# Scanning the last turn of a batch in two halves of positions, in a hybrid of selective scan, attention and experts

## The chip, the cores and the metric

The kernel runs on one core of one Trainium2 chip. The metric is the device time of one execution in microseconds (us). Beside it a profile is taken: one execution recorded by the hardware profiler, from which all the views below are answered. The engines are PE (TensorE: matmuls, and PEld for its weight loads), DVE (VectorE), ACT (ScalarE), POOL (GpSimd) and SP (SyncE, which here issues nearly all DMAs).

## The reference

The input x is 4 x 384 x 32 x 32 (batch, channels, height, width). Layer 0 is a selective scan in four directions over the 1024 positions; layer 1 is windowed causal attention and a mixture of four experts, of which each token takes two.

```
xs = _cross_scan(gn(x))          # 4 directions: rows, columns, and both reversed
h  = h * exp(dt * A) + (dt * u) * B_t     # per channel, 16 states, over 1024 positions
y  = sum over states of h * C_t
x  = x + gelu(layernorm(y0 + y2 reversed + (y1 + y3 reversed) transposed))
t  = tokens of x                 # 4 x 1024 tokens of 384
t  = t + attention(ln(t))        # 6 heads, causal, the last 64 positions
t  = t + experts(ln(t))          # softmax gate, top 2 of 4, 384 -> 1536 -> 384
```

A token needs y at its position from all four directions of its batch. It does not need y at later positions.

## The kernel before, in words

**Order of instructions.** Nothing is ordered by hand. Every stage is a Python generator that yields either a condition or an instruction (lines 137 to 204). `Machine` (218 to 382) runs all of them in a modelled time, with a cost for each instruction, and emits the instructions of each engine in the order in which its model would start them; `bias` makes a stage early (-6 us) or late (+6 us). On the chip each engine then runs its own list in that order and waits for semaphores.

**The scan.** One (batch, direction) is a *turn*, `turns` at 562: 16 turns, four per batch, in the order of directions 1, 3, 0, 2 (`ORDER`, 560; odd ones go by columns, 2 and 3 are reversed). The 384 channels are three tiles t of 128, each four groups j of 32; 32 channels x 4 states fill the 128 partitions. A *block* is (turn, t, j), 12 per turn, and a block has four groups g of states. So there are 48 *slots* per turn and 768 in all, taken by pairs of blocks (`place_of`, 574). A slot is

- `times_b` (814): POOL multiplies dt*u (tile dtus) by B (tile bcs) into z, 128x1024;
- `decay` (830): ACT makes dA = exp(a * dt), in PSUM, two buffers;
- `scan` (856): DVE runs `tensor_tensor_scan` along the 1024 positions, into z or into dA;
- `times_c` (843): POOL or DVE, whichever the model has freer, multiplies by C into z;
- `fold_y` (890), once per two blocks: PE sums the states with a matrix of ones (`fold`) into a PSUM bank, and the 128x512 result is added to what lies in DRAM (`ydr`, laid out as tile t, group j, 64 rows of half and channel, 512 positions).

`spread` (804) loads dt and dt*u from DRAM (`dtr`, four buffers) with each row repeated for four states; `time_steps` (764) makes them on PE, ACT and DVE some 40 slots ahead; `state_rows` (752) loads B and C.

**The tokens.** `tokens(b)` (967) handles eight tiles of 128 tokens, three at a time, with four weight buffers of 576 KB (of the eight that the experts also use) and row buffers out of ten. It starts when `layer1` (1516) sees ("scan", b), which `fold_y` sets after the batch's last fold (927). A tile loads its rows of y (991) and x, and goes through two normalizations, q/k/v, attention, projection, a third normalization, and the gate's logits.

**The experts.** `routes` (1521) sorts each half batch (four token tiles) to experts: `route` (1212) scatters rows by indirect DMA; a half batch becomes 5 or 14 tiles of 128 rows (`SIZES`, 43), 19 a batch. `loads`, `hidden`, `gelus` and `output` (1371 to 1451) run these tiles in order: weights in 576 KB pieces, `ps_hid` and `y_ff` matmuls. `combine` (1464) gathers and adds. All of it is spawned late.

So scans of batch b+1 run beside tokens and experts of batch b, on the same in-order engines; after the last scan only the tokens and experts of batch 3 and what is left of batch 2's experts remain.

Of the kernel before, what the change touches and what calls it, by code (L numbers as in the profile page):

```python
# [11 lines left out]
F32 = mybir.dt.float32  # L12
AF = mybir.ActivationFunctionType
ALU = mybir.AluOpType
# [3 lines left out]
P = 128  # L18
B, D, HH, WW = 4, 384, 32, 32
L = HH * WW  # L20
T = D // P
HB = 512
NH = L // HB
KG, NS, R = 4, 16, 12
# [4 lines left out]
JB = P // 32  # L29
NB = T * JB  # L30
SG = 4
NG = NS // SG
# [7 lines left out]
PT = NT // 2  # L40
# [18 lines left out]
def bcast(ap, n):  # L59

    return ap.unsqueeze(1).to_broadcast([ap.shape[0], n, ap.shape[1]])
# [331 lines left out]
def conv_attn_hybrid(  # L393
# [8 lines left out]
    const = ctx.enter_context(tc.tile_pool(name="const", bufs=1))  # L402
# [77 lines left out]
    count_p = const.tile([P, SEG], F32, name="count_p")  # L480
    base_e = const.tile([P, NE], F32, name="base_e")
    a4 = const.tile([P, KG, T, JB, NG], F32, name="a4")

    m = Machine(nc)
    ps_a = ctx.enter_context(tc.tile_pool(name="ps_a", bufs=1, space=PSUM))
# [65 lines left out]
    ydr = [dram.tile([T, JB, P // 2, LH], F32, tag="ydr", name="ydr") for _ in range(B)]  # L551
# [5 lines left out]
    wl2 = dram.tile([NE, NCH, P, HT * D], F32, name="wl2", bufs=1)  # L557
    pwl = dram.tile([P, T * D], F32, name="pwl", bufs=1)

    ORDER = (1, 3, 0, 2)  # L560
    LAST_BY_COLUMNS = 3
    turns = [(b, ORDER[ki]) for b in range(B) for ki in range(KG)]
    blocks = [(i, t, j) for i in range(len(turns)) for t in range(T) for j in range(JB)]
    NSLOT = len(blocks) * NG
    SP = 2 * NG
    TS, IS = JB * NG, NB * NG
    AHEAD = 3
    xds, dtws, bcs, dtrs, spreads = {}, {}, {}, {}, {}
    zs, das, ready = {}, {}, set()
    have = set()  # L570
    count_of = dict(scan=0, times=0)
    pe, act, dve, pool, sp = m.pe, m.act, m.dve, m.pool, m.sp

    def place_of(s):

        return s // SP * 2 + s % 2, s % SP // 2

    def scans(n):
        return lambda: count_of["scan"] >= n
# [184 lines left out]
    def time_steps():  # L764

        for i, (b, k) in enumerate(turns):
            for t in range(T):
                yield lambda: i in xds and ("u", b) in have and count_of["scan"] >= (i * T + t) * TS - 40
                u = yield from us_all.take("ub")
                yield from sp.dma_start(u, udr[b][t])  # L770


                dtr = dram.tile([2, P, L], F32, tag="dtr", name="dtr", bufs=4)
                bias = dtb_sb[:, k, t : t + 1]
                for h in range(NH):
                    c, r = ts(h, HB), slice(32 * h, 32 * h + R)
                    e, dt = yield from eds.take("ed", n=2)
                    w = yield from banks.take("ps_dt", 0)
                    yield from pe.matmul(w, dtws[i][r, ts(t, P)], xds[i][r], start=True, stop=True)
                    yield from act.activation(e, w, AF.Abs, bias=bias)  # L780
                    yield from act.activation(dt, w, AF.Relu, bias=bias)
                    yield from act.activation(e, e, AF.Exp, scale=-1.0)
                    yield from act.activation(w, e, AF.Identity, bias=1.0)
                    yield from dve.scalar_tensor_tensor(e, w, -1.0, e, ALU.add, ALU.subtract)
                    yield from act.activation(w, w, AF.Ln)
                    yield from dve.tensor_tensor(w, w, e, ALU.subtract)
                    yield from dve.tensor_tensor(w, w, dt, ALU.add)
                    if k % 2:
                        v = slice(h * (WW // NH), (h + 1) * (WW // NH))
                        yield from dve.tensor_tensor(  # L790
                            e.rearrange("p (w h) -> p w h", h=HH),
                            w.rearrange("p (w h) -> p w h", h=HH), colmajor(u)[:, v, :], ALU.mult,
                        )
                    else:
                        yield from dve.tensor_tensor(e, w, u[:, c], ALU.mult)
                    yield from act.copy(dt, w)
                    banks.give(w)
                    yield from sp.dma_start(dtr[1][:, c], e)
                    yield from sp.dma_start(dtr[0][:, c], dt)
                    eds.give(e, dt)  # L800
                us_all.give(u)
                dtrs[i, t] = dtr

    def spread(c):

        for n, (i, t, j) in enumerate(blocks):
            yield lambda: (i, t) in dtrs
            dst = yield from (dtus if c else dts).take("dts")
            yield from sp.dma_start(
                dst, dtrs[i, t][c, 32 * j : 32 * j + 32, :].unsqueeze(1).to_broadcast([32, SG, L])  # L810
            )
            spreads[n, c] = dst

    def times_b():
        for s in range(NSLOT):
            n, g = place_of(s)
            i = blocks[n][0]
            yield lambda: (
                (n, 1) in spreads and (i, g, 0) in bcs and s <= count_of["scan"] + AHEAD
            )  # L820
            z = yield from zs_.take("z", 0)
            yield from pool.tensor_tensor(z, spreads[n, 1], bcs[i, g, 0], ALU.mult)
            zs[s] = z
            count_of["times"] += 1
            if g == NG - 1:
                dtus.give(spreads.pop((n, 1)))
            if n % NB == NB - 1:
                bs_.give(bcs.pop((i, g, 0)))

    def decay():  # L830
        for s in range(NSLOT):
            n, g = place_of(s)
            i, t, j = blocks[n]
            yield lambda: (n, 0) in spreads
            da = yield from das_.take("dA")
            yield from act.activation(
                da, spreads[n, 0], AF.Exp, scale=a4[:, turns[i][1], t, j, g : g + 1]
            )
            das[s] = da
            if g == NG - 1:  # L840
                dts.give(spreads.pop((n, 0)))

    def times_c(s, h, on_pool):
        n, g = place_of(s)
        i = blocks[n][0]
        yield lambda: (i, g, 1) in bcs
        if on_pool:
            yield from pool.tensor_tensor(zs[s], zs[s], bcs[i, g, 1], ALU.mult)
        else:
            yield from dve.tensor_tensor(zs[s], h, bcs[i, g, 1], ALU.mult)  # L850
            das_.give(h)
        if n % NB == NB - 1:
            cs_.give(bcs.pop((i, g, 1)))
        ready.add(s)

    def scan():

        for s in range(NSLOT):
            n, g = place_of(s)
            i = blocks[n][0]  # L860
            yield lambda: s in zs and s in das
            z, da = zs[s], das.pop(s)
            on_pool = count_of["times"] >= min(s + AHEAD, NSLOT) and m.clock["pool"] < m.clock["dve"] + LEAD
            h = z if on_pool else da
            if turns[i][1] >= 2:
                yield from dve.tensor_tensor_scan(
                    h[:, ::-1], da[:, ::-1], z[:, ::-1], 0.0, ALU.mult, ALU.add
                )
            else:
                yield from dve.tensor_tensor_scan(h, da, z, 0.0, ALU.mult, ALU.add)  # L870
            count_of["scan"] = s + 1
            if s % SP == 0:
                m.spawn(fold_y(n), EARLY)
            if on_pool:
                das_.give(da)
                m.spawn(times_c(s, h, True))
            else:
                yield from times_c(s, h, False)
        ended.append(True)
        yield lambda: len(das_.free) == 2  # L880
        for n in range(2):
            banks.free.append(das_.free.pop(0))
        for stock, n in ((zs_, NZ), (dts, 4), (dtus, 4)):
            yield lambda: len(stock.free) == n
            rows.free += stock.free
            stock.free = []
# [3 lines left out]
    def fold_y(n):  # L890


        i, t, j = blocks[n]
        b, k = turns[i]
        rows_y = ydr[b][t, j : j + 2].rearrange("j r l -> (j r) l")
        prev = yield from yps.take("yp")
        yield from sp.dma_start(prev, rows_y)
        ps = None
        for g in range(NG):
            s = n // 2 * SP + 2 * g  # L900
# [22 lines left out]
        banks.give(ps)  # L923
        yield from sp.dma_start(rows_y, prev)
        yps.give(prev)
        folded[b] = folded.get(b, 0) + 2
        if folded[b] == KG * NB:
            have.add(("scan", b))

    folded = {}  # L930

# [35 lines left out]
    def tokens(b):  # L967
# [3 lines left out]
        scale = 1.0 / float(np.sqrt(HD))  # L971
        p = rp.tile([P, NT, NE], F32, tag="p", name="p", bufs=B)
# [11 lines left out]
        wp = yield from weights("wp", pwl.rearrange("p (t o) -> p t o", t=T))  # L984

        def tile(a):
            w = yield from rows.take("yl")
            tt = yield from rows.take("tt")
            hf, r = divmod(a, NT // 2)
# [525 lines left out]

    def layer1():
        for b in range(B):
            yield lambda: ("scan", b) in have
            yield from tokens(b)

    def routes():
# [76 lines left out]
```

## Time and profile before

| what | us |
|---|---|
| median of 3 runs | 3890.63 (3870.85 to 3907.89) |
| the profiled execution | 3882.5, span 3880.8 |
| PE busy | 3033.4 (78%) |
| DVE busy | 2940.7 (76%) |
| POOL busy | 2824.4 (73%) |
| ACT busy | 2226.8 (57%) |
| start of the last scan | 3201.87 |
| mean granted TensorE clock | 0.822 |

Busy shares are means over stages that differ; a share of 78% says little by itself. The page cuts the span into 40 slices of 97 us, and the windows view gives each engine's busy time in any stretch, also for one tile's instructions alone. A group's line gives its busy time, the mean duration of one in ns, and the idle time of its engine just before it with what ended that.

Two numbers of batch 1 (batches are counted from 0 here) help to follow the text. In the timeline its token tiles' first loads (yl) are issued at 1597 us and its fourth token tile's logits stand at 1938.10.

### The profile page before, as it was taken

What the parts mean: (1) busy time and instruction counts of PE and PEld (TensorE: products, weight loads), DVE (VectorE), ACT (ScalarE), POOL (GpSimd) and SP (SyncE); (2) the same over time, 40 slices, a digit from 0 to 9 for tenths busy, and PEclk for the clock granted to TensorE, in tenths of its full rate; (3) what the DMA queues carried; (4) which work ended last, traced back from release to release, by engine and by line L of the source; (5) the groups of instructions that cost most, each with busy time, mean ns of one, the idle gap of its engine ahead of it and who ended that gap; (6) DMA issues with size and microseconds to landing.
All of it is one profiled execution on the core that took longest, in us unless ns stands there. A gap on an engine that the chain in (4) does not pass through costs nothing. (4 is left out here: it accounts for less than half of the span.)

```text
span 3880.8 us, 50273 instructions
## 1 busy us (share of the span) xinstructions
PE 3033.4 (78%) x15868; PEld 1841.7 (47%) x15868; DVE 2940.7 (76%) x3358; ACT 2226.8 (57%) x4017; POOL 2824.4 (73%) x1474
## 2 busy tenths in 40 slices
PE   2555555577697988777768889899787899998997
PEld 1100010045464555344345545566555557876886
DVE  2999999998888998888888899988788992332001
ACT  2545454467586777755557767778675763432221
POOL 1999989988898877888888699889787981012001
PEclk6555556678798999876678989899898999998997
DMA  5775775544478998734357989776568975459995
GB/s 202 266 273 204 270 268 203 174 143 149 171 253 333 341 374 324 285 127 164 112 208 254 329 301 347 270 254 213 203 228 295 388 272 184 136 167 327 318 318 182
DMA packets 394145, 953.65 MB, mean 246 GB/s; under 512 B 49620, under 2 KB 173400, under 8 KB 393880
## 3 DMA queue, kind: packets, MB, share of 16 engines
q1 hardware_dynamic: 385688, 925.27, 68.1%
q0 software_dynamic: 8192, 25.17, 1.9%
q8 instruction: 126, 2.06, 0.2%
q14 instruction: 139, 1.14, 0.1%
HBM read 786.39 MB, written 182.78 MB: 250 GB/s over the span
## 5 line engine op out<-in xcount | busy, mean ns | idle before, releaser
L148 POOL TENSOR_TENSOR z<-dts,bc 128x1024 f32<-128x1024 f32 x768 | 1792.9, 2359 | 186.7 <-PE ps_y L159 105.8
L148 ACT ACTIVATE dA<-dts,a 128x1024 f32<-128x1024 f32 x768 | 854.6, 1118 | 536.8 <-DVE z L148 512.1
L159 PE MATMUL ps_y<-z,fold 128*32 128x512 f32 x3072 | 725.8, 765 | 436.2 <-POOL z L148 237.2
L148 DVE TENSOR_TENSOR_SCAN dA<-dA,z 128x1024 f32<-128x1024 f32 x409 | 935.6, 2288 | 93.2 <-ACT dA L148 77.7
L148 POOL TENSOR_TENSOR z<-z,bc 128x1024 f32<-128x1024 f32 x359 | 841.7, 2355 | 110.8 <-DVE z L148 96.2
L148 DVE TENSOR_TENSOR_SCAN z<-dA,z 128x1024 f32<-128x1024 f32 x359 | 807.8, 2276 | 31.6 <-ACT dA L148 28.6
L159 PEld LDWEIGHTS ps_hid<-xbt,w_sb 128*128 128x128 f32 x5472 | 667.0, 198 | 137.2 <-issue 38.3
L159 PE MATMUL y_ff<-w_sb,hs 128*128 128x384 f32 x1824 | 680.8, 515 | 58.5 <-ACT hs L159 46.4
L159 PE MATMUL ps_hid<-xbt,w_sb 128*128 128x128 f32 x5472 | 692.0, 284 | 33.1 <-ACT hs L148 8.2
L148 DVE TENSOR_TENSOR z<-dA,bc 128x1024 f32<-128x1024 f32 x409 | 499.1, 1220 | 13.8 <-DVE dA L148 0.5
L159 PEld LDWEIGHTS ps_y<-z,fold 128*32 128x32 f32 x3072 | 93.1, 120 | 872.8 <-POOL z L148 412.8
L148 ACT ACTIVATE hs<-ps_hid,bb 128x128 f32<-128x128 f32 x912 | 274.1, 365 | 391.8 <-PE ps_hid L159 320.2
L159 PEld LDWEIGHTS y_ff<-w_sb,hs 128*128 128x128 f32 x1824 | 341.3, 199 | 314.9 <-issue 65.9
L148 POOL DMA_INDIRECT cb<-ysdr,idx x64 | 62.6, 979 | 293.7 <-DMA ysdr<-yb 269.8
L159 POOL TENSOR_TENSOR rn<-rn,half 128x1 f32<-128x1 f32 x96 | 52.7, 549 | 266.7 <-DVE rn L159 209.0
L148 DVE COPY yb<-y_ff 128x384 f32<-128x384 f32 x22 | 12.2, 556 | 251.5 <-PE y_ff L159 204.9
L148 POOL DMA_INDIRECT xsdr<-tks,idx x64 | 65.2, 1018 | 146.5 <-DVE idx L159 58.4
L148 ACT ACTIVATE ed<-ps_dt,dtb_sb 128x512 f32<-128x512 f32 x192 | 125.8, 681 | 67.6 <-PE ps_dt L148 59.8
L148 PE MATMUL ps_dt<-xd,dtw_sb 12*128 12x512 f32 x192 | 136.7, 822 | 24.7 <-DMA dtw_sb<-in_dtw_dram 14.2
L148 DVE TENSOR_TENSOR ps_dt<-ps_dt,ed 128x512 f32<-128x512 f32 x192 | 132.6, 690 | 12.3 <-ACT ps_dt L148 9.5
L148 ACT COPY ed<-ps_dt 128x512 f32<-128x512 f32 x96 | 56.0, 584 | 124.8 <-DVE ed L148 124.5
L304 ACT ACT_TABLE_LOAD x80 | 102.6, 1283 | 2.2 <-PEq L1583 0.8
(204 smaller groups left out, 3411.2 us busy)
## 6 DMA issues: line engine op xcount, KB each, us to landing
w_sb<-wl SPq DMA_DIRECT2D x608, 576.0 KB
dts<-dtr SPq DMA_DIRECT2D x384, 512.0 KB
bc<-xdr SPq DMA_DIRECT2D x128, 512.0 KB
dtr<-ed SPq DMA_DIRECT2D x192, 256.0 KB
ub<-udr SPq DMA_DIRECT2D x48, 512.0 KB
yp<-ydr SPq DMA_DIRECT2D x96, 256.0 KB
ydr<-yp SPq DMA_DIRECT2D x96, 256.0 KB
wl<-in_w_dram SPq DMA_DIRECT2D x32, 576.0 KB
```

The lines of the kernel that those rows point to most:

```text
L148: return getattr(self.real, op)(*a, **k)
L159: getattr(self.real, op)(*a, **k)
L304: self.nc.scalar.add_instruction(mybir.InstLoadActFuncSet(name=self.nc.get_next_instruction_name(), act_func_set_id=EXP_LN_SET,))
```

## The change

Direction 2 becomes the third turn of a batch and direction 0, which runs forward by rows, the last. In turns 7, 11 and 15 (the last of batches 1, 2 and 3, the second to fourth) a block is no longer one group j over 1024 positions. It is two groups j and j+1 over one half of the positions; the first six blocks of the turn take positions 0 to 511 of all channels, the last six positions 512 to 1023. The number of slots, the size of the z and dA tiles, the products and the folds stay. Scans and activations of such a slot come in two instructions of 512. The last position of each first-half scan is copied to a `carry` tile, from which the second half's scan starts. The tokens of positions 0 to 511 (tiles 0 to 3) wait for the first half's folds alone, those of tiles 4 to 7 for the second half's. Batch 0 stays whole.

```
+    carry = [const.tile([P, 2 * NG], F32, name=f"carry{n}") for n in range(NB // NH)]
...
-    ORDER = (1, 3, 0, 2)
+    ORDER = (1, 3, 2, 0)
...
+    halves = [(c, t, j) for c in range(NH) for t in range(T) for j in range(0, JB, 2)]
...
+    halved = (7,11,15)
...
+    def what(n):
+
+        i, t, j = blocks[n]
+        if i not in halved:
+            return i, None, t, j
+        return i, *halves[n - i * NB]
+
+    def pairs(ap):
+
+        return ap.rearrange("p (o l) -> p o l", o=2)
+
+    def rows_of(i, g, c, hf):
+
+        bc = bcs[i, g, c]
+        return bc if hf is None else bcast(bc[:, ts(hf, HB)], 2)
+
+    def view(ap, hf):
+
+        return ap if hf is None else pairs(ap)
+
+    def kept(n, g):
+
+        return carry[n % NB % (NB // NH)][:, 2 * g : 2 * g + 2].unsqueeze(2)
...
     def time_steps():
...
-                yield lambda: i in xds and ("u", b) in have and count_of["scan"] >= (i * T + t) * TS - 40
+                first = i * IS + t * TS // (2 if i in halved else 1)
+                yield lambda: i in xds and ("u", b) in have and count_of["scan"] >= first - 40
...
     def spread(c):
...
+            else:
+                for o in range(2):
+                    r = slice(32 * (j + o), 32 * (j + o) + 32)
+                    yield from sp.dma_start(
+                        dst[:, ts(o, HB)],
+                        dtrs[i, t][c, r, ts(hf, HB)].unsqueeze(1).to_broadcast([32, SG, HB]),
+                    )
...
     def decay():
...
+            for o in range(1 if hf is None else 2):
+                c = slice(0, L) if hf is None else ts(o, HB)
+                yield from act.activation(
+                    da[:, c], spreads[n, 0][:, c], AF.Exp,
+                    scale=a4[:, turns[i][1], t, j + o, g : g + 1],
+                )
...
     def times_c(s, h, on_pool):
...
+        eng = pool if on_pool else dve
+        if hf == 0:
+            yield from eng.tensor_copy(kept(n, g), pairs(h)[:, :, HB - 1 : HB])
+        yield from eng.tensor_tensor(view(zs[s], hf), view(h, hf), rows_of(i, g, 1, hf), ALU.mult)
...
     def scan():
...
+            if hf is not None:
+                for o in range(2):
+                    c = ts(o, HB)
+                    initial = kept(n, g)[:, o, :] if hf else 0.0
+                    yield from dve.tensor_tensor_scan(h[:, c], da[:, c], z[:, c], initial, ALU.mult, ALU.add)
...
     def fold_y(n):
...
+        else:
+            rows_y = ydr[b][t, :, 32 * hf : 32 * hf + 32, :]
...
-        folded[b] = folded.get(b, 0) + 2
-        if folded[b] == KG * NB:
-            have.add(("scan", b))
+        key = b, hf
+        folded[key] = folded.get(key, 0) + 1
+        whole = (KG - (i // KG * KG + KG - 1 in halved)) * NB // 2
+        for c in range(NH):
+            if folded[b, None] == whole and (whole == KG * NB // 2 or folded.get((b, c), 0) == NB // 4):
+                have.add(("scan", b, c))
...
         def tile(a):
+            yield lambda: ("scan", b, a // PT) in have
...
     def layer1():
         for b in range(B):
-            yield lambda: ("scan", b) in have
+            yield lambda: ("scan", b, 0) in have
```

More of the change, by code (lines that the diff above doesn't have):

```diff
@@ L804, in spread @@
     def spread(c):
-        for n, (i, t, j) in enumerate(blocks):
+        for n in range(len(blocks)):
+            i, hf, t, j = what(n)
             yield lambda: (i, t) in dtrs
             dst = yield from (dtus if c else dts).take("dts")
-            yield from sp.dma_start(
-                dst, dtrs[i, t][c, 32 * j : 32 * j + 32, :].unsqueeze(1).to_broadcast([32, SG, L])
-            )
+            if hf is None:
+                yield from sp.dma_start(
+                    dst, dtrs[i, t][c, 32 * j : 32 * j + 32, :].unsqueeze(1).to_broadcast([32, SG, L])
+                )
+            else:
+                for o in range(2):
+                    r = slice(32 * (j + o), 32 * (j + o) + 32)
+                    yield from sp.dma_start(
+                        dst[:, ts(o, HB)],
+                        dtrs[i, t][c, r, ts(hf, HB)].unsqueeze(1).to_broadcast([32, SG, HB]),
+                    )
             spreads[n, c] = dst
@@ L816, in times_b @@
             n, g = place_of(s)
-            i = blocks[n][0]
+            i, hf, *_ = what(n)
             yield lambda: (
@@ L821, in times_b @@
             z = yield from zs_.take("z", 0)
-            yield from pool.tensor_tensor(z, spreads[n, 1], bcs[i, g, 0], ALU.mult)
+            yield from pool.tensor_tensor(
+                view(z, hf), view(spreads[n, 1], hf), rows_of(i, g, 0, hf), ALU.mult
+            )
             zs[s] = z
@@ L832, in decay @@
             n, g = place_of(s)
-            i, t, j = blocks[n]
+            i, hf, t, j = what(n)
             yield lambda: (n, 0) in spreads
             da = yield from das_.take("dA")
-            yield from act.activation(
-                da, spreads[n, 0], AF.Exp, scale=a4[:, turns[i][1], t, j, g : g + 1]
-            )
+            for o in range(1 if hf is None else 2):
[3 more added lines that the diff above has]
+                    scale=a4[:, turns[i][1], t, j + o, g : g + 1],
+                )
             das[s] = da
@@ L844, in times_c @@
         n, g = place_of(s)
-        i = blocks[n][0]
+        i, hf, *_ = what(n)
         yield lambda: (i, g, 1) in bcs
[L847 to L850, printed above, removed]
+        eng = pool if on_pool else dve
+        if hf == 0:
+            yield from eng.tensor_copy(kept(n, g), pairs(h)[:, :, HB - 1 : HB])
+        yield from eng.tensor_tensor(view(zs[s], hf), view(h, hf), rows_of(i, g, 1, hf), ALU.mult)
+        if not on_pool:
             das_.give(h)
@@ L859, in scan @@
             n, g = place_of(s)
-            i = blocks[n][0]
+            i, hf, *_ = what(n)
             yield lambda: s in zs and s in das
@@ L864, in scan @@
             h = z if on_pool else da
-            if turns[i][1] >= 2:
+            if hf is not None:
[3 more added lines that the diff above has]
+                    yield from dve.tensor_tensor_scan(h[:, c], da[:, c], z[:, c], initial, ALU.mult, ALU.add)
+            elif turns[i][1] >= 2:
                 yield from dve.tensor_tensor_scan(
@@ L890, in fold_y @@
     def fold_y(n):
-        i, t, j = blocks[n]
+        i, hf, t, j = what(n)
         b, k = turns[i]
-        rows_y = ydr[b][t, j : j + 2].rearrange("j r l -> (j r) l")
+        if hf is None:
+            rows_y = ydr[b][t, j : j + 2].rearrange("j r l -> (j r) l")
+        else:
+            rows_y = ydr[b][t, :, 32 * hf : 32 * hf + 32, :]
         prev = yield from yps.take("yp")
```

## The prediction

> **What bounds the kernel now.** I read the page's table of slices first, to find the stages; then the windows view over stretches cut where the expert stage (tile y_ff) begins and pauses; then the same windows for y_ff alone; then the groups, for prices.
>
> The slices (one digit is a tenth of busy share in 97 us):
>
> ```profile
> PE   2555555577697988777768889899787899998997
> ...
> DVE  2999999998888998888888899988788992332001
> ...
> POOL 1999989988898877888888699889787981012001
> PEclk6555556678798999876678989899898999998997
> ```
>
> Up to slice 33 VectorE and GpSimd are full: that is the scan, 768 slots, whose last scan starts at 3201.87 us. After it both fall to 0 to 3 and PE stays at 9. So the program is a scan bound by VectorE and GpSimd, then a tail bound by PE. The tail is as long as the expert and token work that PE could not do beside the scan, so the question is where PE lacked work earlier. The windows (length, then busy us of each engine, clock, DMA share, GB/s):
>
> ```profile
> core 0: us, PE busy (x) PEld busy (x) DVE busy (x) ACT busy (x) POOL busy (x), PEclk, DMA share, GB/s
> 1620.00:2030.00 410.00, 292.94 (x1310) 162.59 (x1310) 354.38 (x451) 241.48 (x432) 360.56 (x201) 0.68 0.44 149
> ...
> 3204.00:3520.00 316.00, 299.21 (x1979) 246.84 (x1980) 106.22 (x437) 132.33 (x354) 34.05 (x64) 0.97 0.55 178
> 3520.00:3836.00 316.00, 304.02 (x1824) 241.55 (x1823) 19.75 (x38) 72.44 (x240) 17.61 (x18) 0.97 0.88 305
> ```
>
> and for y_ff alone (24 matmuls are one expert tile of 128 rows):
>
> ```profile
> 1036.00:1620.00 584.00, 175.53 (x456) 87.64 (x456) 0.00 (x0) 9.18 (x19) 0.94 0.87 319
> 1620.00:2030.00 410.00, 0.00 (x0) 0.00 (x0) 0.00 (x0) 0.00 (x0) 0.68 0.44 149
> 2030.00:2430.00 400.00, 100.12 (x264) 49.92 (x264) 0.00 (x0) 5.26 (x11) 0.91 0.86 309
> 2430.00:2910.00 480.00, 83.62 (x216) 41.81 (x216) 0.53 (x1) 3.84 (x8) 0.91 0.68 232
> 2910.00:3204.00 294.00, 92.31 (x240) 45.14 (x240) 0.00 (x0) 4.73 (x10) 0.94 0.87 318
> 3204.00:3520.00 316.00, 78.53 (x216) 39.89 (x216) 2.23 (x4) 2.38 (x5) 0.97 0.55 178
> 3520.00:3836.00 316.00, 150.65 (x432) 76.92 (x432) 9.48 (x17) 0.48 (x1) 0.97 0.88 305
> ```
>
> So the tiles run 19, 0, 11, 9, 10, 9, 18. There is a hole of 410 us without an expert tile: batch 1's (counted from 0) experts end near 2868, batch 0's ended near 1620, and batch 1's tokens could start only when its last fold was written (the first loads of yl stand at 1597). The pace is 36 us a tile in 2030:2430 (400/11), 53 while tokens also run (480/9), 29 beside the scan alone (294/10).
>
> **What the Trainium skill says.** "PSUM — Partial Sum Buffer", section "Engine vs sequencer instructions": ScalarE, VectorE and GpSimd queues are strict FIFO. The trace agrees: rn on POOL sat 266.7 us for DVE's rn, 160.5 of it after 3204, with everything behind it. "TensorE: Matmul & The Clock Gate", section "What's actually happening": the clock is throttled by default, and activity releases it. It agrees: 0.68 in the hole, 0.97 in the tail. "SBUF — State Buffer", section "SBUF: two separate sides": a VectorE operation with two SBUF inputs locks the ports shared with GpSimd. Used in a rival. "Perfetto Trace Analysis", section "Optimizing Scalar/DVE Operations": some 60 ns a VectorE instruction on SBUF, 125 on PSUM, about twice that in profiled latency. The halved scan is not in this trace; this prices it below.
>
> **The change, part by part.** The prices:
>
> ```profile
> L148 ACT ACTIVATE dA<-dts,a 128x1024 f32<-128x1024 f32 x768 | 854.6, 1118 | 536.8 <-DVE z L148 512.1
> ...
> L148 DVE TENSOR_TENSOR_SCAN dA<-dA,z 128x1024 f32<-128x1024 f32 x409 | 935.6, 2288 | 93.2 <-ACT dA L148 77.7
> ...
> L148 ACT ACTIVATE ed<-ed 128x512 f32<-128x512 f32 x96 | 60.3, 629 | 0.1
> ...
> L148 DVE SCALAR_TENSOR_TENSOR cb<-cb,gate,ps_c 128x384 f32<-128x384 f32 x32 | 19.1, 602 | 32.3 <-DMA cb<-ysdr,idx 26.4 <-ACT ps_c L148 5.9
> ```
>
> 1. *Scans in halves.* 3 turns x 48 slots = 144 slots with two scans of 512 for one of 1024. Extra: one fixed cost, 0.06 us (the skill's SBUF figure) to 0.25 (its PSUM figure doubled); I take 0.15: 21.6 us of VectorE (9 to 36).
> 2. *The kept state.* 72 copies of 128x2. On VectorE they cost like total<-ps_r (0.15), on GpSimd like the short rn<-rn (0.19): about 12 us in all. The second half reads them 24 slots later, so nobody waits. Queued behind each copy is only its own product.
> 3. *Decay in halves.* 2 x 629 - 1118 = 140 ns x 144 = 20 us of ScalarE. It is covered by ScalarE's 512 us of idle time before dA; if that cover goes, "scan idle for ACT dA" (now 77.7 + 28.6 us) grows by at most 20.
> 4. *Spread.* 72 more issues on SP's queue x 0.52 us (median issue of dts<-dtr) = 37 us over some 530; dts is loaded up to four blocks ahead. A 2048-byte packet took 84 ns at the median, one of 4096 took 159: 9 ns per pair. Nothing.
> 5. *Time steps* of t=1 and t=2 of a halved turn come 8 and 16 slots sooner, with their ub load, two dtr stores per half, some 7.5 us of ScalarE (12 operations near 0.63) and 6 of VectorE each. Same sum, closer together: nothing, at worst a few us of ScalarE delay. *Order* (k=2 third, k=0 last): the same operations in other turns, nothing. *Fold:* as many transfers of the same size. Nothing.
> 6. *Tokens.* Those of batches 1 to 3 may start after 24 of the last turn's 48 slots. Those turns take 193, 176 and 159 us between first scans, so half is **about 90 us earlier**. Everything a token tile issues moves with it: ten-odd matmul groups on PE, its bn_stats and sums on VectorE, six rn operations on GpSimd (which hold z products behind them while they wait for VectorE), and on SP four weight loads of 576 KB per batch and six transfers per tile. For batches 1 and 2 all this ran beside scans before and still does: it moves, its sum stays. For batch 3 it moves out of the tail into the scan.
>
> *The ledger.* Batch 1's experts start 90 us sooner (1940, not 2030). Their course then repeats the rows above 90 us earlier: 11 tiles, 9 tiles, 10 tiles, so 3114 is where 3204 was. Batch 0's last five tiles now run at 53 instead of 29 us and end near 1740, inside the shortened hole: free. From 3114 to the end of the scan PE gets 90 us plus whatever the scan is lengthened by (d) in the mode "scan, tokens, experts": a tile of experts each 53 us, a tile of tokens each 60 (480 us for eight).
>
> PE's price in the tail: experts 16.4 us a tile (11.8 tiles in 194 us of 3589:3783), tokens about 22 (the token groups of the page sum to 761 us for 32 tiles, 24, mostly at a lower clock). So each us of that mode saves 16.4/53 + 22/60 = 0.68 us of tail.
>
> d: VectorE and GpSimd share the third operation of each slot, so 34 us from 1 and 2 cost half, 17. About two token tiles of batch 3 add some 9 us of VectorE each (106 us in 3204:3520 less two routes and copies) and rn on GpSimd, waits included about 1.4 us an operation pair: 11 to 15 us after sharing. With 3's leak, d = 35 (15 to 70).
>
> Sum: -90 x 0.68 + 35 x (1 - 0.68) = -61 + 11 = **-50 us**. Against the profiled 3882.5 that is 3832; the median of the three runs stands 8 above the profiled run, so **3840**. The tail also has 29 us of idle PE (632 - 603), mainly before batch 3's second part is routed. With the first part's five tiles ready sooner 10 to 20 of it may go; I leave this in the range. Late next is PE itself: the rest of batch 2, tokens 2 to 7, then 14 tiles of the second part at 16.4.
>
> **Rivals.**
> - *More comes.* Token phases overlap with experts better than the old rows say, d is 15 and the tail's idle goes: -61 + 5 - 20 = -76, or -100 if batch 1's tokens, slowed before by batch 0's combine (cb runs 1649 to 2145 on the same row buffers), get away before it. 3790 to 3815. For: batch 2's first four tokens took 237 us, batch 1's 309. Chance 0.25.
> - *The forecast,* 3820 to 3850. Chance 0.35.
> - *Tokens start but do not get on.* They now meet batch 0's experts, hold four of eight weight buffers and up to ten rows; the first route comes hardly sooner. Then half of the 61 or nothing is left: 0 to -30, 3860 to 3890; this is also what a patchwork of a newly planned order would hide. Against: batch 2's tokens ran beside experts and were the faster ones. Chance 0.22.
> - *The halved scan waits (slower).* The second half's scan reads z and its start value from SBUF. If that counts as two SBUF inputs, it waits for GpSimd's product in flight (2.36 us, on average 1.2): 72 slots x 2 scans x 1.2 to 2.4 = 170 to 340 us of d, each costing 0.32 net: +54 to +109, less 50: +4 to +59, 3895 to 3950. It decides from d = 190, where 61 is spent. Against: cb<-cb,gate,ps_c also takes a start-like value and a row from SBUF and the rest from PSUM; it took 586 to 608 ns with GpSimd working and 614 without. A milder form, tokens queued in front of scans in three more half turns so that scan and fold starve each other, gives the same sign. Together 0.18.
>
> That the change does not do what it says is excluded: the wait names the half, and the first half's folds come before it.
>
> **The numbers.** 1% of the median is 39 us, about what a measurement here can tell from none. Faster by more (below 3852): 0.25, nearly all of 0.35 and some of the third case, 0.6. Within 1%: 0.23. Slower: 0.17. The range takes the gains to -110 and the third case and the start of the slow one: 3780 to 3910; the likeliest case alone is 3815 to 3860.
>
> **What would show it.** Scans of 128x512, 288 of them at 1.15 to 1.3 us; the window without y_ff shrinking from 410 to about 200 us; batch 1's first route near 1850 instead of 1940; the last scan near 3237; about 22 to 23 expert tiles and 6 token tiles after it instead of 27 and 8. Wrong if scans of halves exceed 1.5 us, if the last scan lies past 3300, if the hole stays, or if PE after the last scan is idle for more than some 40 us.

## The result and the profile after

The changed kernel took 3866.47 us at the median of six runs (3862.32 to 3872.71), the kernel before beside it 3889.43: a ratio of 0.9948 with a 95% interval of 0.9925 to 0.9970. That is 23 us where 50 were forecast. The profiled execution has a span of 3862.4 us, 18.4 less than before. Below, a *tail* is what follows the last scan, the *backlog* is what is left of batch 2's expert tiles at that time, and an expert tile *leaves* when its result is copied out of PSUM (the yb copy).

The page's slices of the changed kernel:

```profile
PE   2555555587797898976886787898878988988997
...
DVE  2999999998888887788888897878888987342001
...
POOL 1999999998898877898997777888988997020001
PEclk8555556678797899987897798989988999988997
```

The dip of PE in the middle is shorter, and the scan reaches into a 34th slice. The windows of y_ff, cut again where the experts begin and pause, show both (the columns are those of the prediction):

```profile
1036.00:1685.00 649.00, 177.62 (x456) 88.67 (x456) 0.00 (x0) 9.06 (x19) 0.90 0.83 293
1685.00:1895.00 210.00, 0.00 (x0) 0.00 (x0) 0.00 (x0) 0.00 (x0) 0.73 0.50 167
1895.00:2400.00 505.00, 125.59 (x312) 61.50 (x312) 0.00 (x0) 6.24 (x13) 0.87 0.82 287
2400.00:2880.00 480.00, 83.07 (x216) 41.18 (x216) 0.00 (x0) 4.33 (x9) 0.91 0.70 238
2880.00:3270.00 390.00, 121.33 (x312) 59.61 (x312) 0.00 (x0) 6.24 (x13) 0.90 0.83 295
3270.00:3405.00 135.00, 25.14 (x72) 12.90 (x72) 1.12 (x2) 0.48 (x1) 0.96 0.42 127
3405.00:3490.00 85.00, 3.38 (x6) 1.90 (x6) 0.00 (x0) 0.00 (x0) 0.82 0.52 168
3490.00:3818.00 328.00, 156.57 (x451) 80.44 (x450) 8.91 (x16) 1.43 (x3) 0.97 0.86 296
```

The hole without a tile has shrunk from 410 to 210 us. When the scan ends, at 3267 now, 3 + 19 expert tiles are left, where before it was 27. That is the number of tiles that the prediction gave as a sign (22 to 23), and batch 2's experts end at 3405 instead of 3495. But then there is a new pause, 3405:3490, with a quarter of one tile in 85 us. All engines in these two windows of the changed kernel:

```profile
3270.00:3405.00 135.00, 134.10 (x917) 113.13 (x917) 52.67 (x225) 69.30 (x192) 8.44 (x21) 0.96 0.42 127
3405.00:3490.00 85.00, 75.87 (x470) 65.94 (x469) 30.64 (x103) 33.74 (x90) 28.93 (x38) 0.82 0.52 168
```

PE is busy 89% of the pause, though with hardly any expert work. It runs mainly the small matmuls of batch 3's tokens and of batch 2's `combine`, at a clock of 0.82, while nearly all of the next work in quantity, batch 3's experts, waits for those tokens and their route. The first token tile of batch 3 ends at 3300 in both kernels and the last at 3502 and 3503: its earlier start, beside a longer scan, brought nothing. Ninety us of backlog were won, and the end came 18 us sooner: the last expert tile leaves at 3817.4, before at 3835.6.

What the halves cost, from the groups of the changed kernel kept apart by shape:

```profile
L148 DVE TENSOR_TENSOR_SCAN dA<-dA,z 128x512 f32<-128x512 f32 x96 | 117.7, 1226 | 18.1 <-issue 8.6 <-POOL carry L148 5.6 <-ACT dA L148 2.2
L148 DVE TENSOR_TENSOR_SCAN z<-dA,carry,z 128x512 f32<-128x512 f32 x78 | 95.2, 1266 | 3.2 <-ACT dA L148 3.2
L148 DVE TENSOR_TENSOR_SCAN dA<-dA,carry,z 128x512 f32<-128x512 f32 x66 | 84.9, 1287 | 23.0 <-ACT dA L148 11.8 <-issue 10.4
L148 DVE TENSOR_TENSOR_SCAN z<-dA,z 128x512 f32<-128x512 f32 x48 | 55.2, 1202 | 6.0 <-ACT dA L148 6.0
L148 DVE COPY carry<-dA 128x2 f32<-128x2 f32 x48 | 7.5, 157 | 1.4
...
L148 ACT ACTIVATE dA<-dts,a 128x512 f32<-128x512 f32 x288 | 197.7, 691 | 64.0 <-DVE z L148 59.8
```

In these lines "issue" is idle time for which the view names no releaser. A pair of half scans takes 2.40 to 2.57 us for 2.28 whole, as priced. A pair of decays takes 2 x 691 ns for 1118, 264 more instead of the 140 that the row of 629 had promised. Unlike that row the decay reads its scale from SBUF and writes to PSUM; which of the two makes the 62 ns was not separated.

VectorE from 1385 us, where turn 7 begins, to the end of the last scan, in the kernel before and in the changed kernel (the columns are those of the windows in the prediction):

```profile
1385.00:3204.16 1819.16, 1513.57 (x8216) 944.47 (x8215) 1579.63 (x1685) 1235.27 (x2210) 1572.41 (x795) 0.87 0.73 259
```

```profile
1385.00:3268.60 1883.60, 1562.98 (x8771) 1006.90 (x8770) 1614.52 (x1893) 1315.86 (x2472) 1603.92 (x841) 0.88 0.76 263
```

Of the 64 us by which the stretch is longer, 35 are more work of VectorE and some 30 are more idle time. The idle time put down to ScalarE does not grow in the views (125 us before, 123 after), but that is partly a matter of names. All 11 waits of scans put down to "issue" there, 19 us together, ended within 0.16 us after a decay of ScalarE, and so did the two put down to "POOL carry". One of them:

```profile
1398.63 1.23 DVE L148 TENSOR_TENSOR_SCAN dA<-dA,z 128x512 f32<-128x512 f32 x1 [2.26 <-issue]
```

The two decays of this slot ended at 1397.82 and 1398.54, so the first scan of the pair started right after the second decay. Counted so, some 23 of the 30 us are waits for ScalarE's decays and time steps.

### The profile page after: what moved, and what is told of

Its sections match the earlier page's. It is cut to its first block, busy times and chain, and to the rows that moved or that the text cites. A ratio compares the mean times of both kernels' runs of the same rounds, so it can differ in the third digit from the quotient of the medians.

```text
span 3862.4 us, 50744 instructions
## 1 busy us (share of the span) xinstructions
PE 3007.7 (78%) x15862; PEld 1846.8 (48%) x15862; DVE 2955.1 (77%) x3516; ACT 2283.1 (59%) x4213; POOL 2856.6 (74%) x1510
## 5 line engine op out<-in xcount | busy, mean ns | idle before, releaser
L148 ACT ACTIVATE dA<-dts,a 128x1024 f32<-128x1024 f32 (+1 forms) x912 | 892.8, 983 | 504.0 <-DVE z L148 474.1
L159 PE MATMUL ps_y<-z,fold 128*32 128x512 f32 x3072 | 695.8, 762 | 398.1 <-POOL z L148 221.3
L148 POOL TENSOR_TENSOR z<-z,bc 128x1024 f32<-128x1024 f32 x371 | 870.8, 2357 | 95.6 <-DVE z L148 85.9
L148 DVE TENSOR_TENSOR_SCAN dA<-dA,z 128x1024 f32<-128x1024 f32 (+1 forms) x412 | 840.5, 2040 | 86.6 <-ACT dA L148 54.3
L148 DVE TENSOR_TENSOR_SCAN z<-dA,z 128x1024 f32<-128x1024 f32 (+1 forms) x356 | 748.5, 2131 | 33.8 <-ACT dA L148 30.0
L159 PEld LDWEIGHTS ps_hid<-xbt,w_sb 128*128 128x128 f32 x5472 | 686.6, 203 | 142.1 <-issue 46.6
L159 PE MATMUL y_ff<-w_sb,hs 128*128 128x384 f32 x1824 | 692.7, 522 | 66.5 <-ACT hs L159 57.9
L159 PE MATMUL ps_hid<-xbt,w_sb 128*128 128x128 f32 x5472 | 709.1, 289 | 42.7 <-DMA w_sb<-wl 12.7
L148 DVE TENSOR_TENSOR z<-dA,bc 128x1024 f32<-128x1024 f32 x397 | 483.9, 1219 | 11.5 <-DVE dA L148 0.5
L148 DVE SCALAR_TENSOR_TENSOR ed<-ps_dt,ed 128x512 f32<-128x512 f32 x96 | 65.1, 679 | 60.9 <-ACT ps_dt L148 60.6
```

The lines of the kernel that those rows point to most:

```text
L148: return getattr(self.real, op)(*a, **k)
L159: getattr(self.real, op)(*a, **k)
```

## The experiments

The theories at the start: **A**, the prediction's ledger with terms of the wrong size; **B**, the end is set by batch 3's tokens, so that halving turn 15 is worth nothing; **C**, a newly planned order of all instructions is itself worth as much as the change. D came after the second group. All runs, each with its ratio to the kernel before on the same chip, and from its profile in us: the last scan's start, the end of batch 2's experts, the first and the last expert tile of batch 3 (ends of the yb copies).

| run | ratio (95%) | last scan | batch 2's end | batch 3 first, last |
|---|---|---|---|---|
| before | 1 | 3202 | 3495 | 3511, 3836 |
| after | 0.9948 (0.9925 to 0.9970) | 3267 | 3405 | 3506, 3817 |
| e1_order_only | 0.9986 (0.9969 to 1.0002) | 3190 | 3484 | 3499, 3823 |
| e2_halved_late_tokens | 1.0109 (1.0084 to 1.0134) | 3257 | 3546 | 3563, 3887 |
| e3_halved_7_11 | 0.9942 (0.9925 to 0.9960) | 3255 | 3301 | 3501, 3823 |
| e4_halved_15 | 1.0009 (0.9997 to 1.0020) | 3235 | 3513 | 3556, 3851 |
| f1_halved_7 | 0.9991 (0.9976 to 1.0006) | 3220 | 3420 | 3512, 3826 |
| f2_one_decay | 1.0172 (1.0148 to 1.0196) | 3241 | 3564 | 3578, 3900 |
| f3_whole_ops | 1.0020 (1.0006 to 1.0033) | 3195 | 3487 | 3504, 3827 |
| f4_costs_in_plan | 1.0003 (0.9987 to 1.0019) | 3293 | 3456 | 3499, 3826 |
| g1_before_4tiles | 1.0020 (1.0006 to 1.0033) | 3208 | 3506 | 3555, 3852 |
| g2_7_11_4tiles | 0.9922 (0.9896 to 0.9948) | 3257 | 3304 | 3493, 3807 |
| g3_after_4tiles | 0.9944 (0.9927 to 0.9961) | 3276 | 3439 | 3504, 3820 |
| g4_7_4tiles | 0.9946 (0.9927 to 0.9965) | 3222 | 3476 | 3502, 3818 |
| h1_before_5_less | 0.9860 (0.9837 to 0.9884) | 3199 | 3270 | 3459, 3772 |
| h2_7_11_5_less | 0.9931 (0.9912 to 0.9950) | 3259 | 3196 | 3504, 3818 |
| h3_whole_scans | 1.0112 (1.0089 to 1.0135) | 3230 | 3527 | 3549, 3872 |
| h4_no_state | 1.0051 (1.0033 to 1.0069) | 3254 | 3451 | 3544, 3857 |

### Parts of the change alone

```
e1    halved = ()
e2    halved = (7,11,15);  tile(a) and layer1:  yield lambda: ("scan", b, 1) in have
e3    halved = (7, 11)
e4    halved = (15,)
```

> Order of directions 1, 3, 2, 0 as in the changed kernel, no turn halved, so every batch's tokens wait for its last fold as before. Theory A (the gain is PE work moved ahead of the end of the scan, less a longer scan): nothing moves, 3880 to 3895 us, last scan within 10 us of 3202. Theory C (a newly planned order alone is worth as much as the change, 23 us): more than 15 us away from the kernel before, either way, with the stages' ends scattered.

3883.1 us. The new order of directions does nothing that can be told here, and C is not supported: the stages stand some 10 us from where they were (the last scan 12 us earlier, a little more than expected).

> Turns 7, 11 and 15 halved as in the changed kernel, but all tokens of a batch wait for both halves: only the cost of halving is left. Theory A, with the terms of the prediction (34 us of instructions, half of it shared): last scan near 3220, 3890 to 3905 us. If the scan's delay of 65 us in the changed kernel came from the halved instructions themselves (waits for ScalarE's two activations, for the copy, for ports): last scan at 3250 or later, 3920 us or more.

3927.7 us, the second answer. The last scans of e1 and of e2, in the timeline of VectorE (start, length, then the group):

```profile
3190.12 2.29 DVE L148 TENSOR_TENSOR_SCAN z<-dA,z 128x1024 f32<-128x1024 f32 x1 [0.17 <-ACT dA L148]
```

```profile
3248.45 9.50 DVE L148 TENSOR_TENSOR_SCAN z<-dA,carry,z 128x512 f32<-128x512 f32 x8
```

The eight scans of e2 end at 3258, the last one starting at 3257, 67 us after that of e1. So **halving alone costs 67 us of scan** and 1.23% (48 us) of time. The early tokens then win 1.61% (62 us) back, between e2 and the changed kernel. The forecast had 61 for them. It had only 17 for the instructions, and a third of that at the end. The 17 were right as work: from 1385 us to the scan's end VectorE is busy 17 us longer than in e1 (1594 for 1576), and idle 48 us longer (279 for 231).

The longer scan gave PE nothing either. In e1 and e2 alike 27 expert tiles leave after the last scan, batch 2's experts end 16 to 17 us before batch 3's first tile, and that end moved from 3484 to 3546. Batch 1's first tile had already left 71 us later (2140 for 2069), though the scan was only some 20 us behind e1's by then; why was not found.

> Only turns 7 and 11 halved (batches 1 and 2); batch 3's tokens wait for its last fold. Theory A: batch 3's early tokens are a third of the gain; without them 3875 to 3890 us. Theory B (the end is set by batch 3's last token plus some 315 us, and halving turn 15 makes the scan longer by about what it starts the tokens sooner): as fast as the changed kernel or faster, 3850 to 3868 us, batch 3's last token at 3485 to 3505.

3868.2 us: as fast as the changed kernel, at the upper edge of B's numbers and below A's, though the last token came at 3529, later than B had it. Windows of y_ff in e3:

```profile
3255.00:3305.00 50.00, 21.57 (x62) 10.70 (x60) 0.56 (x1) 0.96 (x2) 1.00 0.68 224
3305.00:3460.00 155.00, 0.00 (x0) 0.00 (x0) 0.00 (x0) 0.00 (x0) 0.86 0.28 86
3460.00:3823.00 363.00, 158.30 (x456) 81.56 (x456) 9.48 (x17) 0.96 (x2) 0.97 0.81 280
```

Here batch 2 is finished at 3301, 194 us before it was in the kernel before, and PE has no expert tile for 155 us. All of that backlog, less a scan 53 us longer, was worth 22 us.

> Only turn 15 halved (batch 3); batches 1 and 2 as before. Theory A: the last batch's tokens begin 80 us sooner beside a scan without delay from earlier turns, 3865 to 3880 us. Theory B: nothing is gained, 3885 to 3900 us, batch 3's last token at 3495 or later though its first begins at 3170 or sooner.

3888.1 us, B's answer for the time, though not by B's way: batch 3's tokens did end sooner (3467, not 3495 or later), but the scan ended 33 us later, batch 2's experts 18 us later, at 3513, and batch 3's first tile left 43 us after them.

### What makes halving dear

```
f1    halved = (7,)
f2    e2, and  decay():  for o in range(1): c = slice(0, L)
f3    f2, and one scan of 1024 in halved slots, no copy to carry
f4    after, with  cost = 0.69  for a decay of 512,  1.22 or 1.28  for a scan of 512  in ask()
h3    e2 with f3's scan and both decays
h4    e2 with  initial = 0.0  and no copy to carry
```

> Only turn 7 halved: batch 1's tokens early, batches 2 and 3 as before. If the gain is the shortened hole between batch 0's and batch 1's experts and each halved turn after it only costs its delay of the scan (turn 11 had 177 us whole and 219 to 228 halved): 3845 to 3862 us, last scan near 3225, faster than the changed kernel. If each of turns 7 and 11 brings its own gain: 3872 to 3882 us.

3876.8 us beside 3884.6, a ratio that can't be told from 1: the second answer. With the last scan at 3220 and batch 2's end at 3420 it stands between e1 and e3 in both; turn 11's halving adds to the backlog won and to the scan's delay. With turn 7 alone the hole has in part only moved: batch 1's experts end at 2570, 289 us sooner than in e1, and then, as batch 2's tokens come no sooner, no expert tile follows for 275 us (window of y_ff in f1):

```profile
2570.00:2845.00 275.00, 0.00 (x0) 0.00 (x0) 0.00 (x0) 0.45 (x1) 0.74 0.51 174
```

> As e2_halved_late_tokens (all tokens wait for both halves), but each halved slot's decay is one activation of 1024 with the first group's scale, so the second group's decay is left wrong. If ScalarE's second activation (264 ns a slot, which puts ScalarE behind its plan so that VectorE's time steps wait for it, 26 us before and 49 in e2) is the cost of halving: last scan from 3257 back to 3225 or sooner, 3895 us or less. If the cost is VectorE's pair of scans or the order of blocks: last scan 3245 to 3257, 3915 us or more.

3947.5 us. The last scan came 16 us sooner than in e2, not 32 or more, and the end 14 us later: the new plan put batch 2's experts at 3564. The time says little about decays; the scan's end says that they are not the whole cost. Even that end has to be read with care: the kernels with whole operations (before, e1, f3, g1, h1) have their last scan between 3190 and 3208 by plan and run alone, so differences under some 18 us between single runs can't be told from none.

> As f2_one_decay, and each halved slot is also scanned once over 1024 with no kept state and no copy, so the scan runs across the two groups. Left of the halving are the order of blocks, the split spread loads, the sooner time steps and the folds' rows. If instructions are the cost: the time of e1_order_only, 3878 to 3892 us, last scan near 3200. If the order of blocks and the closer time steps are: 3910 us or more, last scan past 3235.

3893.2 us, last scan at 3195. The order of blocks, the split loads and the sooner time steps cost at most 5 us of scan. The other 62 come with the halved instructions.

> The changed kernel with the measured cost of the halves in the plan: 0.69 us for a decay of 512 (0.615 before), 1.22 and 1.28 us for a scan of 512 (1.18). If in-order waits from a plan that is too short are a good part of the 67 us: last scan 3267 to 3240 or sooner and 3845 to 3860 us. If not: within 10 us of 3866, either way, by a newly planned order alone.

3883.7 us: outside both answers, 17 us above the changed kernel, with a longer scan (3293). Truer costs for the halves in the plan did not remove the waits. The instructions are those of the changed kernel, so a newly planned order alone took back its gain: the intervals, 0.9987 to 1.0019 and 0.9925 to 0.9970, do not meet.

> As e2_halved_late_tokens (all tokens wait for both halves), with two decays of 512 as there, but one scan of 1024 per halved slot, across the two groups, and no kept state and no copy. If VectorE's pair of scans and the copies make the cost of halving (e2's last scan 3257, with whole operations 3195): last scan at 3220 or sooner. If ScalarE's pair does: 3240 or later. Time 3885 to 3930 us, by where its plan puts the experts.

3926.3 us, last scan at 3230: half-way between the two answers. VectorE's work is no longer than in e1 here, yet the scan is 40 us longer. From the waits of VectorE between 1385 and 3190 us, in e1 and then in h3 (sum, times, longest):

```profile
DVE dA L148 <- ACT dA L148: 57.6, 46, 4.5
...
DVE ed L148 <- ACT ps_dt L148: 18.3, 14, 3.2
```

```profile
DVE dA L148 <- ACT dA L148: 77.2, 42, 5.9
...
DVE ed L148 <- ACT ps_dt L148: 32.1, 19, 6.6
```

Both waits for ScalarE grew, together by 33 us (by 26 us against f3, which has the same order of blocks: 65.7 and 17.8 there). In ed<-ps_dt VectorE stands at a time step whose ScalarE half is late, with the scans of the present turn queued behind it. So the 38 us by which the decays grew were not hidden by ScalarE's idle time, whatever part of the 40 us is due to the plan.

> As e2_halved_late_tokens, but the second half's scans start from zero and no state is copied. If the state (the copies on both engines, and the 35 to 85 ns by which a scan that starts from it is longer) is the larger part of VectorE's cost: last scan at 3235 or sooner. If the pair of scans and of decays by itself is: 3245 or later, 3915 us or more.

3904.6 us, some 10 under the answer for pairs, last scan at 3254 as that answer has it. Without start values and copies the scan is 3 us shorter than in e2: a difference that can't be told from none, so the kept state is not the larger part of the cost. Against e1's 3190, decays in pairs alone add 40 us (h3), scans in pairs with their state alone 51 (f2), both 67 (e2): either pair alone is enough for most of it. In each of the three the larger part is idle time of VectorE (41 to 48 us more than in e1), not work. Why f2 has it, with decays that are not longer, was not found.

### Which bound sets the end

Theory **D**: two chains end nearly together. One is PE's backlog of expert tiles. The other runs from the last scan over batch 3's tokens and first route to its first expert tile; from there 19 tiles of some 16.4 us follow in any case.

```
g1, g2, g3, g4   before, e3, after, f1 with
      m.together([tile(a) for a in range(NT)], TILES if b < B - 1 else 4, EARLY)
h1, h2           before, e3 with
      ffn = [... for o in range(SIZES[a0 > 0] - (5 if n == 5 else 0))]
      and  left[b] == sum(SIZES) - (5 if b == 2 else 0)
```

> The kernel before with four of batch 3's token tiles at a time instead of three; nothing else. Theory D (two chains end nearly together: PE's backlog of expert tiles, and the chain from the last scan over batch 3's tokens and first route to its experts; the change shortens only the first): PE's backlog is the later one here, batch 2's experts ending near 3495 when batch 3's could start, so a shorter token chain brings little: 3872 to 3890 us. Theory A (PE alone): the same.

3895.6 us, slightly slower, and above the range of both theories. The last token comes at 3478 instead of 3502, but batch 2's experts are displaced to 3506.

> Turns 7 and 11 halved, as e3_halved_7_11, and four of batch 3's token tiles at a time. There batch 2's experts end at 3301 and batch 3's first tile leaves at 3501. Theory D: the token chain is the bound, so batch 3's first tile leaves 20 to 40 us sooner and the end follows: 3830 to 3852 us. Theory A: PE is the bound, 3860 to 3872 us as e3.

3855.7 us, between the two answers: batch 3's first tile left only 8 us sooner than in e3, at 3493. It is the fastest complete kernel here; its interval and that of the changed kernel overlap (0.9896 to 0.9948, 0.9925 to 0.9970), so it is ahead of the kernel before, and not shown to be ahead of the changed one.

> The changed kernel (7, 11 and 15 halved) and four of batch 3's token tiles at a time. Theory D: 10 to 30 us sooner, 3836 to 3856 us. Theory A: 3860 to 3872 us.

3865.1 us: no gain, against D. Its first four tokens ended at 3401, those of the changed kernel at 3387. They start beside the scan's second half, where four at a time were no faster than three.

> Turn 7 halved, as f1_halved_7, and four of batch 3's token tiles at a time. There batch 2's experts end at 3420. Theory D: a gain until the backlog of PE is met, 10 to 30 us under the 3877 of f1, 3847 to 3867 us. Theory A: 3870 to 3880 us.

3864.5 us, D's answer. The intervals of f1 and g4 do not meet.

> The kernel before with five of batch 2's 19 expert tiles left out (the last five of its second half; their rows are not computed), some 80 us of PE at the tail's 16.4 us a tile. Theory A (the tail is PE's backlog alone): 3800 to 3815 us. Theory D (behind it, some 20 us earlier, stands the chain last scan, batch 3's tokens, first route, experts): only 15 to 35 us, 3850 to 3872 us, batch 3's first tile leaving at 3480 or later.

3826.8 us. Windows of y_ff in h1:

```profile
3200.00:3275.00 75.00, 25.19 (x72) 12.89 (x72) 0.56 (x1) 0.93 (x2) 0.98 0.52 169
3275.00:3440.00 165.00, 0.00 (x0) 0.00 (x0) 0.00 (x0) 0.00 (x0) 0.88 0.32 100
3440.00:3774.00 334.00, 160.62 (x456) 82.18 (x456) 8.92 (x16) 1.44 (x3) 0.97 0.86 295
```

Neither theory had 1.4% (54 us). The pause of 165 us says what stopped it: batch 2's last tile leaves at 3270, and batch 3's first at 3459. That is the token chain of the kernel before laid bare, 260 us after its last scan, and 52 us before the 3511 that PE's backlog had made of it. D is right in kind, and the distance between its bounds is 52 us, not 20.

> Turns 7 and 11 halved, as e3_halved_7_11, with the same five tiles of batch 2 left out. Theory D: the token chain was the bound already, so at most 10 us less than e3's 3868: 3855 to 3870 us. Theory A: 3785 to 3800 us.

3858.0 us, 0.9931 against e3's 0.9942. Windows of y_ff in h2:

```profile
3200.00:3260.00 60.00, 0.00 (x0) 0.00 (x0) 0.00 (x0) 0.00 (x0) 0.59 0.24 77
3260.00:3480.00 220.00, 0.00 (x0) 0.00 (x0) 0.00 (x0) 0.00 (x0) 0.79 0.25 81
3480.00:3820.00 340.00, 159.80 (x456) 82.03 (x456) 8.92 (x16) 1.43 (x3) 0.97 0.85 292
```

The same five tiles, worth 54 us in the kernel before, are worth nothing that can be told here. PE has no expert tile for 280 us, and batch 3's first tile leaves at 3504, as in e3 and as in the changed kernel. It is not without work: in 3260:3480 it is busy for 177 of 220 us, mostly with batch 3's tokens. Whether these matmuls or the waits between the engines set the pace of the token chain was not separated.

So, in outline, the end is the later of two. With the backlog gone, batch 3's first tile leaves 236 to 260 us after the last scan (g2, h2, e3, h1); then come some 315 us of experts and 45 of gathering. For the kernel before the token chain gives 3459 + 313 + 45 = 3817, and its backlog 3881. The changed kernel ends at 3506 + 311 + 45 = 3862: it cut the backlog below the other chain, and pushed that chain back by what it added to the scan. For the changed kernel itself this is inferred from its pause; the tiles were taken out of the kernel before and of e3.

The two bounds are not independent. In f1 and h4 batch 2's experts end some 92 us before batch 3's first tile, and yet that tile leaves 290 us after the last scan, not 236 to 260; in e4 and g1 it leaves 43 to 49 us after batch 2's end, where in the kernel before it was 16. While PE still has experts of batch 2, batch 3's tokens take longer too: the fourth is done 159 us after the last scan in e3 and h2, 181 to 184 in f1, h4 and the kernel before.

## Why the prediction was half right

The miss is one term of the sum. The tail from the last scan to the last tile is 550 us, as the forecast's sum has it (547, 632 less 0.68 x 125). But the scan's extra length d was 65 us instead of 35, and the other 30 us arrived at the end whole, where each was priced at 0.32: the profiled span moved by 18 us, not 50.

1. *The bound* was right for the kernel before, and wrong for what comes next. "Late next is PE itself" failed. After 52 us (h1) the chain from the last scan over batch 3's tokens is next. PE's idle time, which I offered as a sign, could not show it: PE is 89% busy in the pause.
2. *The ledger of tokens* was right for the starts: the hole went from 410 to 210 us (about 200), and the fourth token of batch 1, on which its first route waits, from 1938 to 1795 (route near 1850 instead of 1940). Its agreement at the end is luck in part. The 22 to 23 tiles do not follow from the ledger's own pace: 125 us at 53 us a tile take 27 tiles to between 24 and 25. PE ran five tiles more before the scan's end (22 left), and of batch 3's tokens none of the eight was finished then, instead of two. Nor do the 62 us between e2 and the changed kernel show the 61: between the two batch 2's end moved by 141 us, and the other chain stopped the gain. Turn 15's half point came at 3171, in the kernel before at 3127, and e3 and e4 show that its halving is worth nothing.
3. *The length d of the scan* was mis-sized: 65 us instead of 35, inside its range of 15 to 70. As work of VectorE it was right: 35 us more, where the terms for scans, copies and tokens give 28 to 32 (a pair of scans 0.13 to 0.29 us over a whole one, for 0.15). The failing term is the rest, 3 to 7 us for waits; VectorE's idle time grew by 30. The prediction put the decays at 140 ns a slot (264 measured) and held them "covered by ScalarE's 512 us of idle time". The waits for ScalarE grew by some 23 us all the same. A reason that fits: that idle time stands where ScalarE waits for VectorE to free a dA buffer, not where its work could be done sooner. How much of d the longer decays make is not settled: h3 has a scan 40 us longer with the decays in pairs alone, where I allowed 20, but f2 has 51 with whole decays.
4. *The price of d at the end*, 0.32 us per us, was the costliest error. It supposes that PE works off tiles in the time that the scan is lengthened by. From e1 to e2 the scan grew by 67 us and the profiled span by 63, with as many tiles left, while PE's backlog still was the later bound. Where the token chain binds, a later scan is a later end too.
5. *The rivals.* That the second half's scan waits for GpSimd's ports did not happen: 1262 to 1287 ns beside GpSimd at work, with z and the start value in SBUF. In the changed kernel 91 of these scans ran beside a product of GpSimd for over 95% of their time, 1276 ns on average, and 15 for under 5%, 1277. The Trainium skill's lock for two SBUF inputs ("SBUF — State Buffer", "SBUF: two separate sides") does not cover a start value read this way, as far as these runs show. Tokens did get on: batch 1's first four took 235 us from the first gelu sum, 309 before. One reading of a line was off, without effect on the sum: of the 266.7 us for which rn on GpSimd found its engine idle, 209.0 were for VectorE's rn.
6. *Chance.* e1 and f3 lie within 0.2% of the kernel before with differently planned orders. But f4 lost the changed kernel's gain by its order alone, and f2, with less work than e2, ends 0.6% later: for single plans chance is some 20 us, as much as the gain. That the gain is more than that rests on its coming back in other plans: e3, g2, g3 and g4 lie 0.5% to 0.8% under the kernel before.

Not tried: splitting another turn of batch 3, and a shorter path from a route to its first tile, which took some 60 to 100 us (in e3 from 3429, the first row scattered, to 3501). Why f2's plan delayed batch 2's experts stays open.

## What to carry to other kernels

Before pricing a gain in the resource that binds a tail, find the second chain that ends there and how far behind it is: take out work of the first (h1) and see where the time stops falling. An engine at 90% busy may be at small work while the bulk waits to be released; ask which instructions fill it. A longer stage is time won for the engine beside it only if that engine gets more done in it (in e2 as many tiles were left after 67 us more). And idle time on an in-order engine covers added work only where that work could run while it is idle; look at what ends the idle time before counting on it.

## What the runs showed of the hardware

A scan of 512 f32 took 1.20 to 1.23 us from zero and 1.26 to 1.29 from a start value in SBUF, against 2.28 for 1024; the start value costs some 60 ns, and state copies of 128x2 took 157 ns on VectorE and 185 on GpSimd. An exponential of 512 from SBUF into PSUM with its scale read from SBUF took 691 ns, one within SBUF with a constant scale 629.
